# Layer 2's front taken up sequence by sequence behind layer 1, in a four-layer kernel

## The chip, the core and the metric

The kernel runs on one core of a Trainium2 chip. The metric is device time in microseconds (us) of one execution. The engines are PE (TensorE; PEld is its weight load), DVE (VectorE), ACT (ScalarE), POOL (GpSimd) and SP, which here only issues DMAs.

## The reference

The input `x` is 2 sequences of 1024 tokens with 128 features. Four layers run one after the other. Each takes a layer norm of `x`, gives it to two branches, and adds the product of the two to `x`:

```
n = layernorm(x);  x = x + attn(n) * silu(ffn(n))
```

Layer 0 is a Mamba-2 state space branch with dense experts. Layer 1 is a delta-rule recurrence whose output is normalised again (`o`), times a mixture of 8 experts with a shared expert, two experts per token. Layer 2 is a linear attention, times a branch that holds a causal softmax attention over rotated rows with its own RMS norm and a second mixture of 8 experts. Layer 3 is a state space branch in both directions, times experts. The change concerns the end of layer 1 and the front of layer 2:

```
moe, shared = ...                      # layer 1, per token
x  = x + layernorm(o) * silu(moe + shared)
n  = layernorm(x)                      # layer 2
r  = rope(rms_norm(n) * norm1_w)
Q, K, V = r @ Wq, r @ Wk, r @ Wv       # then softmax attention, causal
```

## The kernel before

All of `x` stays on the chip as 16 tiles of 128 tokens by 128 features. Four tiles are a group, so there are groups 0 to 3: groups 0 and 1 are the first sequence, 2 and 3 the second. `LATE` is the order 0, 2, 1, 3, the first halves of both sequences before the second halves.

The kernel is traced through a scheduler that sets each engine's order from dependences and its own estimate of times, except inside `manual_schedule` blocks, where the named engines keep the order in which the code issues. Every engine executes its queue strictly in order. A pool is a region of memory; a pool that is opened where another stood waits for the older one to be released, as a whole, or tile by tile where it has `reuse_waits="tile"`.

**End of layer 1** (`layer1`, from line 924). Expert blocks of 128 rows go through PE; each result is scattered to memory by an indirect DMA on POOL's queue (line 1399). Between blocks PE runs the recurrence: `delta` for the groups in the order of `LATE`, then `scan` tile by tile for both sequences. `close(g)` (1129) normalises the recurrence's output of a group: stats and a Newton root on DVE (`moments`, 354), four scalings on DVE (1133), two POOL operations (1134, 1135). `shared(g)` (990) is the shared expert of a group: four products on PE, Silu on ACT, a product on DVE (1000), two more products, and a copy to `acc` that alternates between ACT and DVE (`copy`, 320). Last, for each group in the order of `LATE`, `fetch` (1404) loads the scattered results back with two DMAs on SP's queue and adds them with eight scaled additions on DVE (`add_scaled`, 484), ACT takes the Silu, and DVE multiplies and adds into `x` (1156, 1157).

**Front of layer 2** (`layer2`, 1160). Its pools are opened after all of layer 1's are released. POOL multiplies the cosine and sine tables with the norm weights (1204). `normalise` (374) does, for each group, stats on DVE, a root as Sqrt on ACT with a reciprocal on DVE (`rsqrt`, 341), four scalings to `xn` (382), four transposes on PE and a copy to `xT`. Then `Attention.prepare` (1535), for each sequence: a second root for the RMS norm, four scalings on ACT to `xw` (1547), six POOL operations for the rotation of each group (1555 to 1560), transposes and a copy to `xrT`; after that five projections of 128x512 and one small one per group on PE. Each projection is cast on ACT to `high` and combined on DVE (`parts`, 1529 to 1533). `softmax_attention` (1705) first makes constants on DVE (1713 to 1719: two 128x128 casts, two 128x512 casts, four memsets). Its loop has PE's order by hand: `maxima` (1592) on banks `pm`, three of them, reduced by DVE (1619), then scores `psc`, exponentials on ACT and products with the values `pat`. A list of other pieces (`routed`, 1223) is threaded into given steps of this loop, for example `hidden_columns` (1187), four transposes and a copy.

**Layer 3** (`Layer3.front`, 1827) already takes each sequence as layer 2 finishes it, with DVE's order by hand. The changed layer 2 has the same shape.

Of the kernel before, what the change touches and what calls it, by code (L numbers as in the profile page):

```python
# [11 lines left out]
F32 = mybir.dt.float32  # L12
# [8 lines left out]
P = 128  # L21
# [4 lines left out]
G = 4  # L26
# [249 lines left out]
class Kern:  # L276
# [77 lines left out]
    def moments(self, pool, src, n, eps, tag, newton=False):  # L354

        nc = self.nc
        mv = pool.tile([P, n, 2], F32, name=tag + "mv", tag=tag + "mv")
        rs = pool.tile([P, n], F32, name=tag + "rs", tag=tag + "rs")
        for j in range(n):
            st = pool.tile([P, 6], F32, name=tag + "st", tag=tag + "st", bufs=4)  # L360
            nc.vector.bn_stats(st, src(j))
            nc.vector.bn_aggr(mv[:, j, :], st)
        if newton:
            self.newton(pool, rs, mv[:, :, 1], 1.0, eps)
        else:
            self.rsqrt(rs, mv[:, :, 1], 1.0, eps)
        return mv, rs
# [556 lines left out]
def layer1(K, x, xn, xT, w, inp):  # L924
    nc, tc, c = K.nc, K.tc, K.c
    four = [P, G, P]
    with ExitStack() as es:
# [4 lines left out]
        sf = es.enter_context(tc.tile_pool(name="sf1", bufs=4, space=PSUM))  # L932
        K.normalise(pf, sf, x, xn, xT, inp["lists"][0])

        with tc.tile_pool(name="r1", bufs=1) as pr:
            m1, m2, hot = K.top2(pr, K.logits(pr, sf, xT, w["wr"], w["br"], 8), 8)
            d = Dispatch(K, pf, pr, sf, hot, 8, P, inp["lists"])
            w12 = K.pair_softmax(pf, K.lead(pf, m1, m2, d.last))
        pe = es.enter_context(tc.tile_pool(name="e1", bufs=1))
# [44 lines left out]
        t13 = pf.tile([P, 2, 256], F32, name="t13")  # L984
        t2 = pf.tile([P, 2, P], F32, name="t2")
# [4 lines left out]
        def shared(g):  # L990
            rhs = xT[:, g * 512 : (g + 1) * 512]
            hT = pe.tile([P, 2, 512], F32, name="hT")
            for k in range(2):
# [4 lines left out]
                sg = pe.tile([P, 512], F32, name="sg")  # L998
                nc.scalar.activation(sg, pgt, AF.Silu)
                nc.vector.tensor_mul(hT[:, k, :], sg, put)  # L1000
# [4 lines left out]
            K.copy(grp(acc, g), po)  # L1005


        big = lambda n: pa.tile([P, NT, P], F32, name=n)
        kn, qT, WT, TV, AT = big("kn"), big("qT"), big("WT"), big("TV"), big("AT")
# [138 lines left out]
        for g in LATE[NB:]:  # L1148
            close(g)
        for g in range(NG):  # L1150
            shared(g)
        K.table, K.users = None, []
        for g in LATE:
            run(d.fetch(pe, acc, g, w12))
            K.act(grp(acc, g), grp(acc, g), AF.Silu)
            nc.vector.tensor_mul(grp(acc, g), grp(acc, g), grp(o, g))
            nc.vector.tensor_add(grp(x, g), grp(x, g), grp(acc, g))


def layer2(K, x, xn, xT, w, inp, last):  # L1160
    nc, tc, c = K.nc, K.tc, K.c
    four = [P, G, P]
    flat = lambda a: a.rearrange("p a b -> p (a b)")
    with ExitStack() as es:
        keep = es.enter_context(tc.tile_pool(name="k2", bufs=1))
        s = keep.tile([P, NT, P], F32, name="s")
        h = keep.tile([P, NT, P], F32, name="h")
        hT = keep.tile([P, T], F32, name="hnT")
        rs = keep.tile([P, NT], F32, name="rs")
        lg = keep.tile([P, NT, 8], F32, name="lg")  # L1170
        r2 = keep.tile([P, NT], F32, name="r2")
        normed = {}

# [19 lines left out]
        with ExitStack() as e1:  # L1193
            pf = e1.enter_context(tc.tile_pool(name="f2", bufs=1))
            K.phase("sqrt_and_others")
            seqs = [Attention(K, pf, xn, w, h, b) for b in range(NB)]
            ms = keep.tile([P, NT], F32, name="ms")
            with tc.tile_pool(name="sn2", bufs=8, space=PSUM) as sn, tc.tile_pool(name="p2", bufs=1) as pp:

                n1 = w["n1"].rearrange("p (f two) -> p f two", two=2)  # L1200
                turn = {}
                for n, a in (("cos", 0), ("sin", 0), ("cos", 1), ("sin", 1)):
                    turn[n, a] = pp.tile([P, TPB, 64], F32, name=f"{n}{a}")
                    nc.gpsimd.tensor_mul(turn[n, a], w[n], n1[:, :, a].unsqueeze(1).to_broadcast([P, TPB, 64]))
                K.normalise(pp, sn, x, xn, xT, None, ms)
                K.rsqrt(r2, ms, 1.0, 1e-5)
                for a in seqs:
                    a.prepare(pp, sn, ms, turn)
            for rate, log in inp["rates"]:
                nc.scalar.activation(rate, log, AF.Exp)  # L1210
# [3 lines left out]
            K.phase("natural_log_exp_and_others")  # L1214
            with tc.manual_schedule(engines={mybir.EngineType.PE}):
                with ExitStack() as e3:
# [10 lines left out]
                    softmax_attention(K, pf, sm, sc, so, seqs, routed)  # L1227
# [290 lines left out]
class Attention:  # L1518
# [6 lines left out]
    def __init__(self, K, pf, xn, w, h, b):  # L1525
        self.K, self.pf, self.xn, self.w, self.h, self.b = K, pf, xn, w, h, b
        self.mT, self.ao = {}, {}

    def parts(self, pp, dst, src, low):

        high = pp.tile([P, 512], F32R, name="high", tag="high", bufs=2)
        self.K.nc.scalar.copy(high, src)
        self.K.nc.vector.scalar_tensor_tensor(dst, high.bitcast(F32), low, src, ALU.mult, ALU.add)

    def prepare(self, pp, sc, ms, turn):
        K, pf, xn, w, b = self.K, self.pf, self.xn, self.w, self.b
        nc, c = K.nc, K.c
        four = [P, G, P]
        xrT = pp.tile([P, SEQ], F32, name="xrT", bufs=2)
        rs = pp.tile([P, TPB], F32, name="ars", bufs=2)  # L1540
        for g in range(TPB // G):
            tiles = range(b * TPB + g * G, b * TPB + g * G + G)
            gr = rs[:, g * G : (g + 1) * G]
            K.rsqrt(gr, ms[:, tiles.start : tiles.stop], 1.0, 1e-6)
            xw = pp.tile(four, F32, name="xw", bufs=2)
            for j, i in enumerate(tiles):
                nc.scalar.activation(xw[:, j, :], xn[:, i, :], AF.Copy, scale=gr[:, j : j + 1])
            pair = xw.rearrange("p t (f two) -> p t f two", two=2)
            xe, xo = pair[:, :, :, 0], pair[:, :, :, 1]
            at = slice(g * G, g * G + G)  # L1550
            cose, sine, coso, sino = (turn[n, a][:, at, :] for a in range(2) for n in ("cos", "sin"))
            xr = pp.tile(four, F32, name="xr", bufs=2)
            t2 = pp.tile([P, G, 64], F32, name="t2", bufs=2)
            t3 = pp.tile([P, G, 64], F32, name="t3", bufs=2)
            nc.gpsimd.tensor_mul(xr[:, :, :64], xe, cose)
            nc.gpsimd.tensor_mul(t2, xo, sino)
            nc.gpsimd.tensor_sub(xr[:, :, :64], xr[:, :, :64], t2)
            nc.gpsimd.tensor_mul(xr[:, :, 64:], xe, sine)
            nc.gpsimd.tensor_mul(t3, xo, coso)
            nc.gpsimd.tensor_add(xr[:, :, 64:], xr[:, :, 64:], t3)  # L1560
            K.to_feature_major(sc, lambda i: xr[:, i % G, :], xrT, g)
        self.qT = qT = pf.tile([P, 4, SEQ], F32R, name="qT", bufs=2)
        self.kT = kT = pf.tile([P, SEQ], F32R, name="kT", bufs=2)
        self.va = va = pf.tile([P, TPB, 4, 32], F32, name="va", bufs=2)
        nc.gpsimd.memset(va, 0.0)
        nc.gpsimd.memset(va[:, :, :, 8], 1.0)
        for g in range(TPB // G):
            cols = slice(g * 512, (g + 1) * 512)
            pk = sc.tile([P, 512], F32, name="pk", tag="ps")
            K.mm(pk, w["wk"], xrT[:, cols])  # L1570
            self.parts(pp, kT[:, cols], pk, w["klow"])
            for j in range(4):
                pq = sc.tile([P, 512], F32, name="pq", tag="ps")
                K.mm(pq, w["wq"][:, j, :], xrT[:, cols])
                self.parts(pp, qT[:, j, cols], pq, w["qlow"])
            pv = sc.tile([P, G, 32], F32, name="pv", tag="ps")
            for j in range(G):
                i = g * G + j
                K.mm(pv[:, j, :], xrT[:, i * P : (i + 1) * P], w["wv"])
            nc.vector.tensor_copy(va[:, g * G : (g + 1) * G, :, :8], pv.rearrange("p t (g d) -> p t g d", d=8))  # L1580
# [124 lines left out]
def softmax_attention(K, pf, sm, sc, so, seqs, fill):  # L1705
# [6 lines left out]
    shared = {n: pf.tile(s, F32R, name=n + "R") for n, s in (("ident", [P, P]), ("ones", [P, P]), ("nge", four), ("nle", four))}  # L1712
    nc.vector.tensor_copy(shared["ident"], c["ident"])
    nc.vector.tensor_copy(shared["ones"], c["ones"])
    for n in ("nge", "nle"):
        nc.vector.tensor_copy(shared[n], seqs[0].w[n].unsqueeze(1).to_broadcast(four))
    shared["mp"] = [pf.tile(four, F32R, name=f"mp{n}") for n in range(4)]
    for t in shared["mp"]:
# [436 lines left out]
```

## Time and profile before

| | us |
|---|---|
| Runs of the kernel | 1321.91, 1326.75, 1313.99; median 1321.91 |
| The profiled execution | 1326.39, of which the traced span is 1324.6 |
| Busy in the span | PE 1139.9, DVE 886.0, ACT 506.4, POOL 386.9 |
| Mean granted clock of PE | 0.913 of full speed |
| Last expert block of layer 1 on PE | ends at 419.7 |
| Last addition into `x` by layer 1 | starts at 453.3 |
| First statistics of layer 2 | 459.1 |
| First projection of layer 2 | 479.8 |
| First product of the softmax attention | 504.9 |

Times in the trace count from the start of the span. A group of rows gives line, engine, operation, tile names, sizes and count; what stands in brackets is idle time before it and what ended it. PE's products of fp32 operands appear as two records each. A busy share is an average over a stretch; the clock column is the share of full speed that PE was granted.

### The profile page before, as it was taken

The numbers are of one execution on the slowest core, as the hardware profiler recorded it, in microseconds if no ns is written. First come the engines' busy times: TensorE is split into PE (matmuls) and PEld (weight loads), VectorE is DVE, ScalarE is ACT, GpSimd is POOL, SyncE is SP. The second block draws the span as 40 slices with busy tenths as digits, with TensorE's granted clock in tenths as the row PEclk, the third lists the DMA queues.
The fourth block names the chain that finished last, engine by engine and source line by source line (L and its number), as shares of the span: only waits on it lengthen the run. The fifth ranks groups of instructions, "written<-read, shape, count | busy, mean of one in ns | idle before, by whom it ended". The sixth has DMA issues, their size and how long they took to land.

```text
span 1324.6 us, 18595 instructions
## 1 busy us (share of the span) xinstructions
PE 1139.9 (86%) x6689; PEld 767.2 (58%) x6689; DVE 886.0 (67%) x2311; ACT 506.4 (38%) x917; POOL 386.9 (29%) x372
## 2 busy tenths in 40 slices
PE   5599986888899468899999998499999849999997
PEld 2257765887898235444444444377778725555554
DVE  7944367954855976576788644869767388653376
ACT  5633334113212251344555676042442236422321
POOL 0073530045643350000000000134656411343433
PEclk9799985899999766797999999699999969999998
DMA  2000003035443100000000000234344430421110
GB/s 92 1 0 1 1 15 127 1 124 158 127 125 107 32 1 1 0 1 0 1 1 17 1 1 17 76 90 129 100 135 132 130 111 1 95 53 48 34 39 24
DMA packets 37804, 71.27 MB, mean 54 GB/s; under 512 B 5275, under 2 KB 22176, under 8 KB 37328
## 3 DMA queue, kind: packets, MB, share of 16 engines
q1 hardware_dynamic: 30880, 54.83, 13.7%
q0 software_dynamic: 5440, 9.79, 2.9%
q10 hardware_dynamic: 1392, 5.47, 1.2%
q8 instruction: 53, 0.87, 0.3%
q14 instruction: 39, 0.32, 0.1%
HBM read 62.58 MB, written 8.85 MB: 54 GB/s over the span
## 4 chain that ended last, share of the span: by engine, by line
PE 66%; DVE 18%; issue 7%; ACT 5%; DMA 2%; POOL 2%; ACTq 0%; SPq 0%; DVEq 0%; POOLq 0%; another core or an unknown queue 0%
PE pm L329 6%; PE psc L329 4%; PE pat L329 4%; PE p L329 4%; DVE mx L1619 4%; PE po L329 3%; PE px L329 3%; PE pgt L329 3%; PE pcum L329 3%; PE psh L329 2%; PE put L329 2%; PE pU L329 2%; PE pd L329 1%; PE pTT L329 1%; PE py L329 1%
## 5 line engine op out<-in xcount | busy, mean ns | idle before, releaser
L1619 DVE TENSOR_REDUCE mx<-pm 128x1 f32<-128x512 f32 (+3 forms) x304 | 185.5, 656 | 76.2 <-PE pm L329 71.7
L1389 POOL DMA_INDIRECT xb<-xs,dfrom x85 | 85.2, 1002 | 503.0 <-PE psum L329 348.3
L292 ACT ACTIVATE pr<-psc 128x1024 f32<-128x1024 f32 x144 | 139.6, 1021 | 101.3 <-PE psc L329 69.1
L329 PE MATMUL pm<-kT,qT 32*128 32x128 f32 (+3 forms) x576 | 110.5, 370 | 7.5 <-DVE mx L1619 6.7
L329 PEld LDWEIGHTS pm<-kT,qT 32*128 32x128 f32 x576 | 68.1, 206 | 78.8 <-DVE mx L1619 51.9
L1399 POOL DMA_INDIRECT ys<-yb,dto x85 | 87.4, 1028 | 81.9 <-DVE yb L1279 50.5
L329 PE MATMUL p<-xbT,tw 128*128 128x256 f32 x368 | 99.7, 387 | 4.5 <-ACT sg L1272 2.6
L329 PE MATMUL pat<-pr,va 128*32 128x512 f32 x576 | 80.9, 634 | 0.9 <-DVE ao L326 0.9
L1272 ACT ACTIVATE sg<-p,tw 128x256 f32<-128x256 f32 x92 | 41.0, 471 | 91.2 <-PE p L329 75.8
L329 PEld LDWEIGHTS p<-xbT,tw 128*128 128x128 f32 x368 | 62.8, 192 | 15.4 <-ACT sg L1272 4.3
L329 PE MATMUL psc<-qT,kT 32*128 32x512 f32 x288 | 64.2, 492 | 3.8 <-ACT pr L292 3.8
L1273 DVE SCALAR_TENSOR_TENSOR hh<-p,tw,sg 128x256 f32<-128x256 f32 x92 | 42.5, 478 | 34.2 <-ACT sg L1272 22.4
L2060 POOL TENSOR_TENSOR hT<-hT,gb 128x512 f32<-128x512 f32 x32 | 41.7, 1303 | 75.9 <-DVE hT L2058 67.1
L329 PEld LDWEIGHTS po<-tw,hh 128*128 128x128 f32 x368 | 54.7, 193 | 9.5 <-issue 4.0
L329 PE MATMUL po<-tw,hh 128*128 128x128 f32 x368 | 56.6, 278 | 0.5 <-DVE hh L1273 0.4
L2058 DVE TENSOR_TENSOR hT<-hT,put 128x512 f32<-128x512 f32 x36 | 24.5, 683 | 47.0 <-PE put L329 46.4
L329 PE MATMUL psc<-mT,onesR 32*128 32x512 f32 x288 | 54.6, 419 | 0.0
L338 PE MATMUL tp<-w_c,xn 128*128 128x128 f32 x48 | 14.5, 412 | 46.7 <-DVE xn L382 46.7
L669 POOL TENSOR_TENSOR uda<-w_c,vdA 128x512 f32<-128x512 f32 x24 | 27.1, 1142 | 88.3 <-PE pd L329 40.8
L292 ACT ACTIVATE hT<-pgt 128x512 f32<-128x512 f32 x36 | 21.3, 596 | 78.5 <-PE pgt L329 70.7
L329 PEld LDWEIGHTS psc<-qT,kT 32*128 32x128 f32 x288 | 31.0, 189 | 16.4 <-ACT pr L292 13.4
L338 PEld LDWEIGHTS tp<-w_c,xn 128*128 128x128 f32 x48 | 8.7, 188 | 53.3 <-DVE xn L382 27.6
(540 smaller groups left out, 2740.5 us busy)
## 6 DMA issues: line engine op xcount, KB each, us to landing
tw<-in_rows SPq DMA_DIRECT2D x23, 836.0 KB
tw<-in_rows SPq DMA_DIRECT2D x39, 384.0 KB
gb<-gt SPq DMA_DIRECT2D x32, 256.0 KB
yt<-ys SPq DMA_DIRECT2D x16, 256.0 KB
w_l<-in_l ACTq DMA_DIRECT2D x1, 1890.0 KB
w_e<-in_e SPq DMA_DIRECT2D x1, 1536.0 KB
xb<-xs,dfrom POOLq DMA_INDIRECT x85
ys<-yb,dto POOLq DMA_INDIRECT x85
```

What stands on the lines that cost most here:

```text
L292: op = self.nc.scalar.activation(out, in_, func, **kw)
L329: op = self.nc.tensor.matmul(out, lhsT=lhsT, rhs=rhs, start=start, stop=stop)
L338: self.nc.tensor.transpose(pt[:, j, :], src(g * G + j), self.c["ident"])
L669: pool.tensor_mul(da, upto.unsqueeze(1).unsqueeze(1).to_broadcast(lay), m["dA"][:, i0 + j : i0 + j + per, :].unsqueeze(3).to_broadcast(lay))
L1272: nc.scalar.activation(sg, p1[:, k - k0, :], AF.Silu, bias=t[:, 1536 + k : 1537 + k])
L1273: nc.vector.scalar_tensor_tensor(hh[:, k, :], p2[:, k - k0, :], t[:, 1540 + k : 1541 + k], sg, ALU.add, ALU.mult)
L1389: self.K.nc.gpsimd.indirect_dma_start(dst, None, self.xs, bass.IndirectOffsetOnAxis(self.of_token[:, n : n + 1], 0))
L1399: d = self.K.nc.gpsimd.indirect_dma_start(self.ys, bass.IndirectOffsetOnAxis(self.to[:, n : n + 1], 0), src, None, bounds_check=2 * T - 1, ...
L1619: nc.vector.tensor_reduce(mx[:, starts.index(a), g, j : j + k], tile[0][:, : k * m].rearrange("p (j m) -> p j m", m=m), AX.X, ALU.max)
L2058: nc.vector.tensor_mul(hT, hT, put)
L2060: nc.gpsimd.tensor_mul(hT, hT, gb[k // 2][:, k % 2, :])
```

## The change

- `layer2` becomes a class `Layer2`. Its `front` is called by `layer1` while layer 1's experts' memory (now on the right side of the memory, with `WT` in it) is still held; the recurrence's pools are released before it (`es.close()`). Four PSUM banks (`sf`) stay layer 1's, the other four become the front's ring `sn`.
- Inside `front`, the order of DVE and POOL is the order of the code. Groups are finished in the order 0, 1, 2, 3 instead of 0, 2, 1, 3, and the statistics, roots, turns and projections of the first sequence are issued between the ends of the second sequence's groups.
- `normed` takes the place of `close(g)` for groups 1 and 3: one Newton root for both, the scaling on ACT with a bias, and the two POOL operations.
- Three roots per token (layer norm, its product with the RMS norm, and one for the linear attention) come from one Newton iteration per sequence over 3x8 values on DVE. The Sqrt table is not loaded. `xw` is made on ACT straight from `x`.
- The rotation of group 3 is on DVE instead of POOL. `xw` and `xr` lie in `h`, the tables in `s`, the turned columns in `hT`.
- The attention's constants move from DVE to ACT (casts) and POOL (memsets) and are issued at the start. Copies of `acc` and of the turned columns are all on ACT. `sg` and `high` get one more buffer.
- The 16 transposes of `xn` and their copies to `xT` move into the attention's loop, at steps 8, 12, 16 and 20.
- `moments` gets two buffers, which also concerns the norms at the start of layers 0 and 1.

```diff
-        mv = pool.tile([P, n, 2], F32, name=tag + "mv", tag=tag + "mv")
-        rs = pool.tile([P, n], F32, name=tag + "rs", tag=tag + "rs")
+        mv = pool.tile([P, n, 2], F32, name=tag + "mv", tag=tag + "mv", bufs=2)
+        rs = pool.tile([P, n], F32, name=tag + "rs", tag=tag + "rs", bufs=2)
...
-        for g in LATE[NB:]:
-            close(g)
-        for g in range(NG):
-            shared(g)
+        es.close()
...
+        def normed():
+            gs = LATE[NB:]
...
+            for k, i in sorted(enumerate(tiles), key=lambda a: a[0] % G):
+                st = pe.tile([P, 6], F32, name="lost", bufs=8)
+                yield lambda st=st, i=i: nc.vector.bn_stats(st, o[:, i, :])
+                yield lambda st=st, k=k: nc.vector.bn_aggr(mv[:, k, :], st)
+            yield from K.newton_steps(pe, r, mv[:, :, 1], 1.0, 1e-5)
...
+                nc.scalar.activation(o[:, i, :], o[:, i, :], AF.Identity, bias=b[:, k : k + 1], scale=r[:, k : k + 1])
...
+            def turned(g, by=nc.gpsimd):
+                a = seqs[g * G // TPB]
...
+                    nc.scalar.activation(xw[:, j, :], x[:, i, :], AF.Identity, bias=shift[:, i : i + 1], scale=factors[:, 1, i : i + 1])
+                a.rotate(pp, xr, xw, g * G % TPB, turn, by)
...
+            with tc.manual_schedule(engines={mybir.EngineType.DVE, mybir.EngineType.Pool}):
+                run(chain(shared(0), shared(1), normed()))
+                run(gather(0))
+                run(gather(1))
+                run(shared(2))
+                run(close(0))
+                run(stats(0))
+                run(close(1))
+                run(stats(1))
+                run(roots(0))
+                turned(0)
+                run(shared(3))
+                turned(1)
+                run(gather(2))
+                run(close(2))
+                run(stats(2))
+                run(gather(3))
+                columns(0, sn)
+                low = projected(0, sn)
+                run(islice(low, 1))
+                run(close(3))
+                run(stats(3))
+                run(roots(1))
+                run(islice(low, 3))
+                columns(1, sn)
+                turned(2)
+                run(scaled(0))
+                turned(3, v)
+                run(low)
+                run(projected(1, sn))
+                columns(2, sf)
+                run(projected(2, sf), scaled(1))
+                columns(3, sf)
+                run(projected(3, sf), scaled(2))
+                run(scaled(3))
+                run(second_root())
+            K.users.append(seqs[-1].cast)
+            K.phase("natural_log_exp_and_others")
...
+                    for g in range(NG):
+                        routed.append((8 + 4 * g, lambda g=g: columns(g)))
...
-    nc.vector.tensor_copy(shared["ident"], c["ident"])
-    nc.vector.tensor_copy(shared["ones"], c["ones"])
+    nc.scalar.copy(shared["ident"], c["ident"])
+    nc.scalar.copy(shared["ones"], c["ones"])
...
-        nc.vector.memset(t.bitcast(F32), 0.0)
+        nc.gpsimd.memset(t.bitcast(F32), 0.0)
```

`run` takes steps of the given lists in turn, one of each. `close(g)` in the list is layer 1's last multiplication and addition of a group, `gather(g)` its eight scaled additions and the Silu. `projected(g)` yields six DVE steps (five results, one copy of the values), each after its product on PE and its cast on ACT; `islice(low, n)` takes the next n of them.

## The prediction

> **What bounds the kernel now.** Three rows of the page's 40 slices (33.1 us each) come first: the share of PE, of VectorE (DVE), and the clock granted to PE.
>
> ```profile
> PE   5599986888899468899999998499999849999997
> DVE  7944367954855976576788644869767388653376
> PEclk9799985899999766797999999699999969999998
> ```
>
> Nearly everywhere PE is at 8 or 9. Slices 13 and 14 (430 to 497 us) read 4 and 6; DVE reads 9 and 7 there and the clock drops. That is where layer 1 hands over to layer 2. The table by 10 us stretches (start:end, length, busy PE, PEld, DVE, ACT, POOL, clock, DMA) shows it closer:
>
> ```profile
> 440.00:450.00 10.00, 4.35 (x22) 2.91 (x20) 9.04 (x22) 1.89 (x4) 3.61 (x2) 0.81 0.09 27
> 450.00:460.00 10.00, 0.00 (x0) 0.00 (x0) 8.98 (x24) 1.91 (x2) 6.65 (x6) 0.50 0.00 0
> 460.00:470.00 10.00, 3.22 (x10) 1.81 (x10) 9.69 (x50) 4.09 (x14) 5.33 (x10) 0.50 0.00 0
> 480.00:490.00 10.00, 10.00 (x25) 4.82 (x26) 5.13 (x8) 5.23 (x12) 4.88 (x7) 0.81 0.00 0
> 490.00:500.00 10.00, 9.76 (x41) 5.68 (x40) 7.37 (x12) 5.28 (x10) 0.00 (x0) 1.00 0.01 2
> ```
>
> DVE is full until 470 while PE stands still; then PE carries the four groups' projections at 480 to 504 (the second after the first, all behind the statistics). The waits from 419 to 505 (who waited for whom, us in total, times, longest) and the time line name the works:
>
> ```profile
> PE tp L338 <- DVE xn L382: 23.0, 7, 14.9
> DVE kT L1533 <- ACT high L1532: 6.2, 4, 3.3
> ```
> ```profile
> 455.54 1.49 DVE L1716 CAST nleR<-w_l 128x512 fp32r<-128x512 f32 x1
> 457.08 2.11 DVE L1719 MEMSET mp<- 128x512 f32 x4
> 468.24 2.20 DVE L382 TENSOR_SCALAR xn<-x,lnmv,lnrs 128x128 f32<-128x128 f32 x3
> 468.25 0.73 POOL L1557 TENSOR_TENSOR xr<-xr,t 128x256 f32<-128x256 f32 x1
> 470.36 0.71 DVE L372 TENSOR_TENSOR ms<-ms,lnrs 128x4 f32<-128x4 f32 x1
> 442.68 2.52 POOL L1134 TENSOR_TENSOR WT<-WT,w_l 128x512 f32<-128x512 f32 x1 [12.04 <-DVE WT L1133]
> 504.92 0.70 PE L329 MATMUL pm<-ngeR,identR 128*128 128x512 f32 x2 [0.94 <-DVE va L1580]
> ```
>
> From 453.9 to 459.1 DVE builds the attention's constants, with layer 2's statistics behind them. Beside a running POOL operation a DVE operation of two SBUF inputs, or a TENSOR_SCALAR from SBUF to SBUF, ends only about when POOL's does: xn at 0.73 each instead of 0.28 (the four at 441.49 took 1.11), a 4-column product at 0.71 instead of 0.15. It goes the other way too: 2.52 instead of 1.08 on POOL. The attention's first product is at 504.92, 0.15 after DVE's last `va`. The forecast is when that product comes.
>
> **The change, step by step.** I walk DVE's hand order with durations from this profile; starts next to each other are counted as pitch (a 128x128 operation 0.28, a 128x512 one 0.65, a small dependent one 0.20, four `bn_stats` and four `bn_aggr` 1.2).
>
> 1. Shared experts of groups 0 and 1, four products. The last `put` ends at 429.2 as before (the bank it needs comes free with a copy at 428.1), so DVE is done at 430.0. In between it idles about 3 us: the norms of layer 1's late groups are behind these products by hand, though their rows are there at 425.7.
> 2. `normed`: eight stats-aggr pairs at about 0.42 and 12 small steps: 3.4 + 2.4, to 435.8. The eight scalings leave DVE (8 x 0.28 = 2.2 saved) for ACT, which has room; then four POOL operations of 1.09.
> 3. `gather` of groups 0 and 1: 16 x 0.28 = 4.5. The results landed at 428.8, no wait. POOL's four operations lie beside it. Each can hold one DVE operation (0 to 4 x 0.8 = 3.2); at 428.8 two cost 1.4, at 442.7 one cost DVE nothing. I take 2.1: 442.4.
> 4. Shared group 2 (1.3), twice close and stats (2 x 2.5), 13 root steps (2.6): 451.3. Layer 3's same list took 13 us from 1064.3 to 1077.3, with 1.2 of other work, which fits.
> 5. Shared group 3, `gather`, close, stats, `gather`: 1.3 + 2.25 + 1.3 + 1.2 + 2.25 = 8.3. POOL turns groups 0 and 1 just then, 12 operations at 0.72. Seven adds at 0.72 instead of 0.28 cost 3.1, the close 1.0, the wait for its Silu 0.9: 464.7. Bounds for the port: 0 and 12 x 0.45 = 5.4.
> 6. One projection result (0.8), close (1.3, 0.5 late behind Silu), stats 1.2, roots 2.7: 471.2. POOL is at rest, so the roots run at 0.20.
> 7. Three results (2.4), four scalings beside POOL's turn of group 2 (4 x 0.72), then group 3's turn on DVE, six operations of 128x256 at 0.42 (between the 128x128 and the 128x512 row): 479.0. Group 0's projection used the four `sn` banks meanwhile; PE waits for these results.
> 8. The rest of group 0 (1.1), group 1 (5 x 0.8 + 0.3), group 2 with four scalings (5.4), group 3 at PE's pace (0.86 each) with scalings (6.0): 495.9. ACT's casts (0.58 each) keep up. The last scalings and the second root (1.5) lie beside PE's first products.
>
> The attention's first product comes at 496.2, 8.7 earlier. Gone besides: constants (5.2 of DVE to ACT and POOL, which are free before 430; without that room they would delay the norms by as much), six of twelve 0.65 us DVE copies. The square root table (1.28) sat in an ACT pause and counts nothing. The exp table now comes after the last cast; the first exponential is 26 us later. POOL's queue has its last store at 420.5, ahead of the constants, so no store is held. On SP's queue the loads of the third group's results go out when the first group's tiles are free (438.6) and are wanted at 452.6; a load issued at 422.8 was used at 428.8, so they are in time.
>
> 9. Moved into the attention: 16 transposes and four copies of xT. The nearest row is the same thing at full clock:
>
> ```profile
> 726.75 0.66 PE L1190 MATMUL tp<-w_c,hn 128*128 128x128 f32 x4
> ```
>
> 0.49 until the next product, 1.0 at half clock, and a bank of three held for a copy of 0.58. Low end 2 us for four, high end 4 x 2.1 if PE waits for the bank each time. Steps 8 to 20 lie at about 560 to 610, partly at half clock: +3.
>
> 10. Two buffers for `moments`. Layer 1's start loads ACT tables six times between 203 and 218 as Sqrt and Silu alternate; the second buffer lets a Sqrt come earlier. Two loads fewer are 2.6 and what waits behind; a poorer order costs about 1. Between -4 and +1: -1.
>
> Sum: -8.7 + 3 - 1 = -6.7. The profiled execution took 1326.4 (span 1324.6 and 1.8 around it), so 1319.7 in its place. The median of the runs shown, 1321.9, is 4.5 lower: 1315.
>
> On step 8, the row for a cold start is the first projection: products start 1.7 apart from 479.8 to about 484, then 0.86, so about 2 us are lost after a pause. The sum has that off its path, since PE starts on group 2 at 477 while DVE turns group 3. The Trainium skill's page "TensorE: Matmul & The Clock Gate" (section "Why this matters for your kernels") speaks against this change: it advises no PE gaps above about 3 us between bursts, as one idle window brings half clock back. By that rule groups 0 and 1, now drawn apart by DVE's results, would run at half clock throughout, and group 2 would start so: an estimate from its window of 3.4 us is 1.7 us lost, and the forecast 1317.
>
> **Rivals.**
>
> *The port is free.* If DVE's runs of adds hold the port and POOL is the one delayed, as at 442.68, the 2.1, 4.1 and 1.8 us of steps 3, 5 and 7 fall away: 8.0 more, 1307. Against it: at 468 POOL ran through at 0.73 and DVE lost each time.
>
> *The attention gives it back.* Its clock stood at 0.50 from 590 to 610; PE did 19.6 us of work there that at full clock is 9.8, with DVE and ACT needing about 12. One such stretch more costs up to 8 us: +1, 1323. For it: the added transposes fall just there. Against it: four at 726 left no trace.
>
> *The tail runs at half clock* (slower than before). PE's products wait for four banks that DVE frees late; if the clock never recovers, from 477 come two turns (1.9 each), three products and a v of group 1 (6.8) and two whole groups (10.2 each): 508.1, a cast and a result more 509.7. That is 4.8 late instead of 8.7 early, with 3 and -1 +6.8: 1329. It decides as soon as the first product comes after 502.9. Against it: 24 us of the same products brought the clock to 1.0 within 5 us.
>
> **How the numbers follow.** Forecast (1309 to 1321) 0.40; port free 0.31; attention gives back 0.13; half clock in the tail 0.16. Port free reaches down to 1303 with step 10 at -4 and step 9 at 2, and to 1300 if DVE's pause of 3 us in step 1 closes as well; half clock reaches up to 1337 with step 9 at 8 and the attention's opening (505 to 510, clock 0.76) at 0.50, 2.5 us. 1300 to 1331 leaves out about 0.1 on each side. A measurement of this kernel can tell about 1% (13 us) from no change. Faster than 1308.7: port free and a little of the forecast, 0.34. Slower than 1335: the upper half of the half clock case, 0.08. Within: 0.58.
>
> **What would show it.** First masked product at 493 to 500 instead of 504.9; no constants on DVE; adds of group 2 at about 0.7 each beside POOL's turns, root steps at 0.2; PE clock low from 445 to about 480, then 1.0; the attention itself 2 to 4 us longer. I would be wrong if ACT's or PE's order, which is not by hand, puts a cast that waits for a bank ahead of a Silu or a turn that DVE waits for, or if other stages are ordered anew.

## The result and the profile after

| | before | after |
|---|---|---|
| Median of 17 runs each, us | 1318.96 | 1328.81 |
| Ratio to before, 95% interval | | 1.0062 (1.0038 to 1.0087) |
| Profiled execution, us (span) | 1326.39 (1324.6) | 1329.81 (1328.0) |
| First statistics of layer 1 | 202.2 | 205.8 |
| First expert block on PE | 279.4 | 271.5 |
| Last expert block on PE begins | 417.8 | 421.2 |
| Last copy of the recurrence's `o` begins | 425.5 | 441.7 |
| Last addition into `x` by layer 1 begins | 453.3 | 479.9 |
| First product of the softmax attention | 504.9 | 511.5 |

The change made the kernel slower, by about 8 us in 1319. The forecast was a gain of 6.7 us. That the median still lies between 1300 and 1331 is luck: that range was stretched upward by a rival whose mechanism is not the one found here.

The three rows of the page, now of the kernel after (PE, VectorE, granted clock, 40 slices of 33.2 us):

```profile
PE   5599996889899577899999998589999939999997
DVE  7944358854864896568888653878777378762466
PEclk9798987689999767589999899699999969999999
```

The hole in PE at the hand-over is still there (slices 13 and 14 read 5 and 7), and the clock still falls. The table by 10 us stretches shows that it has moved (columns as in the prediction):

```profile
430.00:440.00 10.00, 10.00 (x61) 7.37 (x60) 4.58 (x19) 3.39 (x7) 0.00 (x0) 1.00 0.14 39
440.00:450.00 10.00, 1.65 (x10) 1.09 (x8) 8.44 (x23) 2.83 (x9) 6.63 (x9) 0.69 0.00 0
450.00:460.00 10.00, 5.96 (x22) 3.88 (x23) 9.71 (x27) 4.54 (x11) 7.41 (x4) 0.62 0.36 106
480.00:490.00 10.00, 5.69 (x15) 3.18 (x14) 9.55 (x33) 4.83 (x11) 3.61 (x7) 0.74 0.00 0
490.00:500.00 10.00, 8.15 (x23) 3.56 (x21) 7.35 (x13) 4.69 (x8) 1.05 (x2) 0.92 0.00 0
```

From 430 to 440 PE is full and DVE is half idle (4.58; the kernel before had 9.69 in these same 10 us): DVE has nothing it may do. Why, the time line says (start, length, engine, line, operation, tiles; in brackets the idle time before and what ended it):

```profile
441.06 1.64 POOL L1833 MEMSET mp<- 128x512 f32 x3 [13.81 <-PE pO L329]
441.69 0.27 ACT L1120 COPY WT<-pO 128x128 f32<-128x128 f32 x1 [0.16 <-PE pO L329]
442.53 0.20 DVE L308 TENSOR_SCALAR nww<-lomv 128x8 f32<-128x8 f32 x1
442.67 5.00 POOL L1216 TENSOR_TENSOR s<-w_l 128x512 f32<-128x512 f32 x4
442.76 1.22 DVE L314 TENSOR_SCALAR lors<-nww 128x8 int32<-128x8 int32 x1
444.01 1.20 DVE L316 TENSOR_TENSOR nwa<-lors 128x8 f32<-128x8 f32 x1
446.49 1.21 DVE L318 SCALAR_TENSOR_TENSOR lors<-nwa,lors 128x8 f32<-128x8 f32 x1
447.73 0.17 DVE L316 TENSOR_TENSOR nwa<-lors 128x8 f32<-128x8 f32 x1
449.01 1.13 DVE L484 SCALAR_TENSOR_TENSOR acc<-yt,rw,acc 128x128 f32<-128x128 f32 x4
511.53 0.70 PE L329 MATMUL pm<-ngeR,identR 128*128 128x512 f32 x2 [1.16 <-DVE va L1697]
```

The recurrence's last output arrives at 441.7, 20.5 behind the last block (before: 7.7). Only then does POOL get the memory in which `s` and `mp` lie, and its four table products run just beside the Newton steps of the late groups, which take 1.2 each until POOL is done and 0.17 after. The norms end at 449.0 (forecast: 435.8). From there to the first product it takes 62.5; the forecast had 60.4.

So the tail that the prediction walked through was nearly as long as forecast, and it began 13 us too late. What has the recurrence, which the diff does not touch, to do with it? Its place in PE's queue. Here are PE's products behind the last one of the last block, in the order in which PE executes them, up to the last `put` (S: products of the recurrence's scan, H: products of the shared experts):

```
before:  H3 S3 H3 S1 H34
after:   H3 S4 H4 S4 H9 S4 H11 S4 H1 S4 H12
```

Four products of the scan are left behind the last block before, twenty after.

**Theories.** A: the second buffer of `moments` (the forecast's step 10) made the scheduler order PE's work in layer 1 anew; the blocks now come ahead of the recurrence, and its end, with all of DVE's hand order, falls late. B: POOL's tables on the recurrence's memory meet the Newton steps whatever the buffers. C: the front gains what was forecast, and the attention or the clock gives it back.

### The profile page after: what moved, and what is told of

Read it like the earlier page. It is cut to its first block, busy times and chain, and to the rows that moved or that the text cites. A ratio compares the mean times of both kernels' runs of the same rounds, so it can differ in the third digit from the quotient of the medians.

```text
span 1328.0 us, 18567 instructions
## 1 busy us (share of the span) xinstructions
PE 1145.9 (86%) x6689; PEld 772.0 (58%) x6689; DVE 884.0 (67%) x2289; ACT 510.3 (38%) x922; POOL 386.2 (29%) x370
## 4 chain that ended last, share of the span: by engine, by line
PE 67%; DVE 19%; issue 6%; ACT 4%; POOL 2%; DMA 1%; SPq 0%; POOLq 0%; ACTq 0%; DVEq 0%
PE pm L329 6%; PE pat L329 4%; PE psc L329 4%; PE p L329 4%; DVE mx L1736 4%; PE px L329 3%; PE po L329 3%; PE pgt L329 3%; PE pcum L329 3%; PE put L329 2%; PE psh L329 2%; PE pTT L329 2%; PE pU L329 2%; PE pd L329 2%; PE pob L329 1%
## 5 line engine op out<-in xcount | busy, mean ns | idle before, releaser
L1518 POOL DMA_INDIRECT xb<-xs,dfrom x85 | 84.7, 996 | 502.5 <-PE psum L329 370.2
L329 PEld LDWEIGHTS psc<-qT,kT 32*128 32x128 f32 x288 | 30.8, 191 | 15.7 <-ACT pr L292 12.7
L329 PE MATMUL pm<-ngeR,identR 128*128 128x512 f32 x64 | 33.4, 544 | 6.7 <-DVE mx L1736 4.1
L324 ACT COPY xbT<-pxb 128x256 f32<-128x256 f32 (+1 forms) x33 | 12.1, 368 | 68.5 <-PE pxb L963 38.9
```

The costliest lines, as they stand in the source:

```text
L324: self.nc.scalar.copy(out, in_)
L329: op = self.nc.tensor.matmul(out, lhsT=lhsT, rhs=rhs, start=start, stop=stop)
L1518: self.K.nc.gpsimd.indirect_dma_start(dst, None, self.xs, bass.IndirectOffsetOnAxis(self.of_token[:, n : n + 1], 0))
```

## The experiments

All are timed in five rounds against the kernel before. Stages are compared from marks in each profile: the last expert block on PE, the last copy of `o`, the end of the late groups' norms, the last addition into `x`, the attention's first product. Experiments 1 to 4 ran on one chip, 5 to 7 on another, 8 and 9, and 10 and 11, on others again. On the first the blocks were quicker (133 to 143 us instead of 137 to 150), so absolute times are held against each other only within these, and distances from the last block across them. One part of these distances goes with the clock and not with the order: from the last addition into `x` to the first product it took 31.6 us at a clock of 0.89 (the kernel after, experiment 1), 33.3 at 0.85 (experiments 4, 5, 7 and 11), 33.1 at 0.80 (10) and 37.4 at 0.77 (3 and 6).

**1. One buffer in `moments`.** The kernel after, less this:

```diff
-        mv = pool.tile([P, n, 2], F32, name=tag + "mv", tag=tag + "mv", bufs=2)
-        rs = pool.tile([P, n], F32, name=tag + "rs", tag=tag + "rs", bufs=2)
+        mv = pool.tile([P, n, 2], F32, name=tag + "mv", tag=tag + "mv")
+        rs = pool.tile([P, n], F32, name=tag + "rs", tag=tag + "rs")
```

> The kernel after with one buffer instead of two in `moments`; nothing else. PE's issue order up to the recurrence's end is then that of before except for a few pieces. Theory A (the second buffer reorders PE in layer 1, the recurrence ends 16 us late, 441.7 instead of 425.5, and the hand order of DVE stands behind it): the last copy of WT at 425 to 428, the norms of the late groups done at 434 to 438, the attention's first product at 495 to 500, and the kernel 4 to 10 us below before (ratio to before 0.992 to 0.997). Theory B (POOL's table products lie on the recurrence's memory and run beside the Newton steps, whatever the buffers): steps still at 1.2 each, first product at 500 to 503, ratio 0.997 to 1.001. Theory C (the gain is lost in the attention or in a low clock): first product at 495 to 500 but the time still at or above before, ratio 1.003 to 1.008.

Measured: 0.9972 (0.9941 to 1.0003), 0.9% below the kernel after. From its time line:

```profile
412.01 0.26 ACT L1120 COPY WT<-pO 128x128 f32<-128x128 f32 x1
412.73 5.04 POOL L1216 TENSOR_TENSOR s<-w_l 128x512 f32<-128x512 f32 x4
416.56 0.29 DVE L1160 BATCH_NORM_STATS2 lost<-WT 128x6 f32<-128x128 f32 x1
420.05 0.17 DVE L314 TENSOR_SCALAR lors<-nww 128x8 int32<-128x8 int32 x1
422.15 1.13 DVE L484 SCALAR_TENSOR_TENSOR acc<-yt,rw,acc 128x128 f32<-128x128 f32 x4
484.30 0.70 PE L329 MATMUL pm<-ngeR,identR 128*128 128x512 f32 x2 [1.16 <-DVE va L1697]
```

The last block begins at 404.4 here. The last copy is 7.6 behind it, the tables pass beside the statistics, which they do not slow, and are over before the Newton steps. The norms end 17.8 behind the last block (forecast 18.0), the first product comes 79.9 behind it (forecast 78.4; before 87.1; after 90.3). Theory A holds; B is a consequence of the late end; C falls for the larger part.

**2. Two buffers in the kernel before.** The same two lines, the other way round, in the kernel before.

> The kernel before with two buffers in `moments`; nothing else. Theory A: the recurrence ends 10 to 16 us later than 425.5, part of it hidden behind the shared experts and the fetches; the kernel 4 to 12 us slower than before (ratio 1.003 to 1.009). Theories B and C: the buffer does what it was forecast to do, 4 us less to 1 us more (ratio 0.997 to 1.001).

Measured: 1.0076 (1.0043 to 1.0110). With the buffer alone, without any of the rest, the kernel is 10 us longer. Its runs also had a lower clock, 0.905 in the mean against 0.916 before, and by the slope in the last section that much clock goes with the whole 10 us; how much is the order itself, and how much a clock that fell with it, was not separated here. In experiments 3 and 10 the clock was only 0.002 lower, worth 1 to 2 us, and 6.6 and 7.8 us were lost, so the order does cost time by itself. Twenty-eight products of the scan are left behind the last block, the last copy is 31.2 behind it (7.7), the first product 94.8 (87.1).

**3. Two buffers in layer 0's norms only.**

```diff
-        K.normalise(pf, sf, x, xn, xT, None, ms)
+        K.normalise(pf, sf, x, xn, xT, None, ms, bufs=2)   # layer 0; everywhere else 1
```

> The kernel after with two buffers in the norms of layer 0 only, one in layer 1. PE's issue order in layer 1 then differs from before (last product of the recurrence 21 places later, as in after) though layer 1's norms have one buffer. Theory A in the form that only the place of the recurrence on PE counts: ends at 435 to 442, ratio to before 1.000 to 1.008. In the form that layer 1's own two buffers are the cause: ends at 425 to 428, ratio 0.992 to 0.997.

Measured: 1.0050 (1.0017 to 1.0082). Layer 1 has its one buffer, and yet twelve scan products are left behind the last block; the last copy is 17.9 behind it, the first product 93.1. (That is later than the 90.3 of the kernel after, although the last addition is earlier, 55.7 instead of 58.7: the stretch behind it is one of the two at a clock of 0.77.) So it is the place of the recurrence that counts, not layer 1's buffer as such: other times for layer 0 are enough to reorder layer 1.

**4. The additions of groups 0 and 1 ahead of the norms.** Two buffers stay.

```diff
-                run(chain(shared(0), shared(1), normed()))
+                run(chain(shared(0), shared(1)))
                 run(gather(0))
                 run(gather(1))
+                run(normed())
```

> The kernel after with the norms of the late groups (`normed`) behind the additions of groups 0 and 1 in DVE's order instead of ahead of them; two buffers stay. Theory A (DVE's order waits for a recurrence that ends at 441.7): the additions (about 4.5 us) run before 442, the norms end at about 449 as before, and all that follows comes 4 us earlier; first product at 506 to 509 instead of 511.5, 2 to 5 us below the kernel after (ratio to before 1.002 to 1.005). Theory C: first product earlier but the time unchanged, ratio 1.006.

Measured: 1.0045 (1.0011 to 1.0079), first product 89.2 behind the last block. The additions did run while DVE waited, and the last addition into `x` came 55.9 behind the last block instead of 58.7; the first product gained 1.1 on the kernel after, less than the 2.5 to 5.5 expected; the stretch behind the last addition had the lower clock (33.3 us at 0.85 against 31.6 at 0.89). The time lies in theory A's range, but its interval covers theory C's 1.006 too and tells neither from the other.

**5. Two buffers in layer 1's norms only.** As experiment 3, with the call in `layer1`.

> The kernel after with two buffers in the norms of layer 1 only, one in layer 0. PE's issue order in layer 1 is that of after but for a few pieces before the first block. If layer 1's second buffer alone is enough (theory A): the recurrence's last copy 20 us behind the last block, as in after (20.5) and not 7.6 as with one buffer; layer 1's first statistics at 202 to 203 (205.8 in after); ratio to before 1.001 to 1.006. If the loss came from layer 0's end (3.4 us later in three of the four runs with two buffers there): last copy near 8 us behind the last block, ratio 0.994 to 1.000.

Measured: 1.0050 (1.0023 to 1.0076); last copy 20.5, first product 91.0 behind the last block. Each of the two places is enough by itself, and that both together (1.0062) cost more can't be seen within these intervals.

This run and experiment 7 shared a chip, so their stages can be laid side by side. First two buffers in layer 1, then one buffer: from layer 1's first statistics to the first block, to the last block, to the attention's first product.

```profile
202.80:267.60 64.80, 50.94 (x264) 45.31 (x265) 52.21 (x183) 18.32 (x47) 6.64 (x8) 0.68 0.29 95
267.60:414.80 147.20, 137.04 (x1149) 131.69 (x1149) 91.14 (x226) 37.07 (x94) 75.25 (x74) 0.99 0.41 124
414.80:505.80 91.00, 62.22 (x242) 37.33 (x240) 69.77 (x194) 37.33 (x78) 32.89 (x39) 0.83 0.08 24
```
```profile
202.50:278.20 75.70, 60.40 (x360) 53.43 (x361) 60.91 (x197) 21.69 (x51) 8.20 (x10) 0.77 0.25 83
278.20:416.20 138.00, 129.52 (x1085) 124.12 (x1083) 83.63 (x220) 36.61 (x96) 73.75 (x72) 0.99 0.42 131
416.20:497.80 81.60, 58.87 (x209) 33.23 (x207) 63.39 (x186) 36.30 (x74) 32.86 (x39) 0.85 0.09 26
```

The number after PE's busy time counts its records: 264 + 1149 + 242 = 1655 against 360 + 1085 + 209 = 1654. It is the same work. With two buffers the blocks start 10.9 us earlier, 96 records ahead of their old place; 64 of these come back between the blocks, which then take 9.2 longer because PE is full there (137.0 of 147.2), and 33 come back behind the last block. To the last block it is 212.0 against 213.7: of the 10.9, 1.7 are left. The tail is 9.4 longer, since what was put off is a chain at the end of which everything waits.

**6. The blocks held back.** Two buffers stay; on PE the blocks' transposes are placed behind the sixth level of the first recurrence round.

```diff
+                if lv == 5 and side == 1 and "mark" not in loaded:
+                    loaded["mark"] = K.latest
...
-                nc.tensor.transpose(pt[:, r, :], xb[:, r, :], c["ident"])
+                op = nc.tensor.transpose(pt[:, r, :], xb[:, r, :], c["ident"])
+                K.behind(op, loaded["mark"])
```

> The kernel after, two buffers as they are, with one order added on PE: the transposes of the expert blocks come behind the sixth level of the first recurrence round, as they do in the kernel before. On PE three scan pieces, not eighteen, are then left behind the first products of the shared experts. Theory A in the form that the loss is the blocks' start ahead of the recurrence: the last copy 7 to 9 us behind the last block, norms done 17 to 19 behind it, ratio to before 0.996 to 1.003 (PE may lose up to 8 us where it now waits with blocks at hand). In the form that the second buffer costs in another way (layer 0, ACT's tables): last copy early but the time still at 1.004 to 1.009.

Measured: 1.0034 (0.9998 to 1.0069). PE's order at the end is that of before (four products left; the counts of three and eighteen in the expectation were short, it is four and twenty), the last copy 7.7 and the first product 84.7 behind the last block. So the place of the blocks makes the late end. The last addition into `x` came 47.3 behind the last block, a little earlier than with one buffer (48.3, experiment 7). That only some 6 of the 9.4 us of the tail came back lies behind that addition, where the order is as in experiment 7 and the clock was lower: 37.4 us at 0.77 instead of 33.3 at 0.85. The first block came 79.6 behind layer 1's first statistics, 3.9 later than with one buffer. In time the run lies between the two and its interval does not decide; of its 8 us against experiment 7, 3.9 are seen there and 3.1 in the tail, and the rest was not found.

**7. One buffer, and the columns of `xT` late.**

```diff
-                        routed.append((8 + 4 * g, lambda g=g: columns(g)))
+                        routed.append((40 + 4 * g, lambda g=g: columns(g)))
```

> The kernel after with one buffer in `moments` and the sixteen transposes of xn with their copies at the attention's steps 40 to 52 instead of 8 to 20. If they cost about 3 us at steps 8 to 20, where PE was granted half clock (the forecast's step 9): 2 to 4 us less than with one buffer alone (0.9972), so 0.994 to 0.996. If they cost nothing there: 0.997. If they lengthen the stretch at half clock (8 us): 0.990 to 0.992.

Measured: 0.9968 (0.9938 to 0.9999), against 0.9972 with the columns early. What they cost at steps 8 to 20 is not measurable: 3 us (0.0023) are not excluded by these intervals, 8 are hardly likely. This version is below before in its interval, barely, and below the kernel after by 0.9%.

**8. The scalings to `xn` on ACT.** On top of experiment 7, the sixteen scalings leave DVE's order.

```diff
-                    yield lambda i=i: v.tensor_scalar(xn[:, i, :], x[:, i, :], mean[b][:, i - b * TPB, 0:1], factors[:, 0, i : i + 1], ALU.subtract, ALU.mult)
+                    nc.scalar.activation(xn[:, i, :], x[:, i, :], AF.Identity, bias=c0[:, i : i + 1], scale=factors[:, 0, i : i + 1])
```

> One buffer in `moments`, the columns of xT late in the attention, and the sixteen scalings to xn taken from DVE's order and made on ACT behind the last cast, where ACT waits some 26 us for its first exponential. If the front is DVE's own work end to end, as the forecast's steps 3 to 8 have it: the four scalings beside POOL's turn (2.95 in the profile with one buffer) leave the path, and part of the twelve others (0.34 each): the first product 3 to 6 us earlier behind the last block (81.6 with late columns, so 76 to 79), ratio to before 0.992 to 0.995. If the front is bound by something else (PE's pace in groups 2 and 3): 81 behind the last block, ratio 0.997.

Measured: 0.9962 (0.9921 to 1.0002); first product 80.9 behind the last block instead of 81.6. Taking some 7 us of work (2.95 and twelve times 0.34 in experiment 1) from DVE shortened the front by 0.7. The time decides nothing, since its interval covers both expectations, but the stages show that my expectation from steps 7 and 8 failed. The four scalings (2.95) did leave DVE's queue, but its next work, the turn of group 3, then waited 1.40 for POOL and took 4.4 beside it instead of 3.4: 0.6 was left. In the second sequence DVE's scalings lay in the gaps between PE's products.

**9. The late groups' statistics between the shared experts' products.** On top of experiment 8.

```diff
-                run(chain(shared(0), shared(1), normed()))
+                rows = normed()
+                run(chain(shared(0), islice(rows, 16), shared(1), rows))
```

> As the run with xn on ACT, and the sixteen statistics of the late groups' norms stand between the products of the shared experts of groups 0 and 1 in DVE's order instead of behind both. DVE idled 3.0 there in the profile with late columns, and the rows were complete 4.4 us before their statistics began. If that place in DVE's order is what the norms wait for: the norms end 2 to 2.5 us earlier behind the last block (17.8 so far), the two first Newton steps beside POOL's tables at 1.2 instead of 0.2, and the ratio is 0.001 to 0.002 below the run with xn on ACT alone. If PE or POOL holds them: no change.

Measured: the norms end 15.7 behind the last block instead of 17.8, and the first product comes 78.9 behind it instead of 80.9: the 2 us went through to the attention. The time does not show them: 0.9995 (0.9961 to 1.0029) beside 0.9962 (0.9921 to 1.0002). Two us are below what these runs resolve.

**10. POOL's tables behind the norms' scalings.** Two buffers stay; the four table products move behind `normed` in POOL's order.

```diff
                 run(chain(shared(0), shared(1), normed()))
+                tables()
```

> The kernel after, two buffers as they are, with POOL's four table products behind the two scalings of the late groups in POOL's order instead of ahead of them. In the profile of after they ran from 442.7 to 447.7, beside the first Newton steps of the late groups' norms, four of which took 1.2 instead of 0.2. If that meeting costs its 4 us: the norms end 23 to 24 behind the last block (27.5 in after, 17.8 with one buffer), the last addition into x 55 to 56 behind it (58.7 and 48.3), ratio to before 1.002 to 1.004. If the tables only hold other DVE work instead (additions, statistics, roots) or delay the first turn: 1.005 to 1.008.

Measured: 1.0059 (1.0029 to 1.0089), as the kernel after. From its time line:

```profile
440.30 0.17 DVE L314 TENSOR_SCALAR lors<-nww 128x8 int32<-128x8 int32 x1
447.79 1.56 DVE L1178 TENSOR_TENSOR acc<-acc,WT 128x512 f32<-128x512 f32 x1
451.76 5.92 POOL L1217 TENSOR_TENSOR s<-w_l 128x512 f32<-128x512 f32 x4
452.22 1.38 DVE L1178 TENSOR_TENSOR acc<-acc,WT 128x512 f32<-128x512 f32 x1 [0.19 <-issue]
453.63 1.67 DVE L1179 TENSOR_TENSOR x<-x,acc 128x512 f32<-128x512 f32 x1
456.52 1.33 DVE L1236 TENSOR_SCALAR nww<-lnmv 128x8 f32<-128x8 f32 x3
```

The Newton steps are at 0.17 and the norms end 23.7 behind the last block instead of 27.8, as expected; the ratio is that of the second case. But the tables now meet the closing of group 1 (1.38 and 1.67 instead of 0.69 each) and the first root steps (three in 1.33 instead of 0.32). The last addition is 57.3 behind the last block (55 to 56 expected), the first product 90.4: the meeting was moved and not removed.

**11. The recurrence first.** Two buffers stay; every product of the shared experts stands behind the scan's last product on PE, and DVE does the norms ahead of them.

```diff
+        K.ahead = K.latest
         follow(sf, shared, normed, gather, finish)
+        K.ahead = None
...
-                run(chain(shared(0), shared(1), normed()))
+                run(chain(normed(), shared(0), shared(1)))
```

> The kernel after, two buffers as they are, with every product of the shared experts behind the recurrence's last product on PE, and the norms of the late groups ahead of the shared experts' products in DVE's order. PE's order up to the last block is unchanged. If the recurrence ends late because products of the shared experts stand between its last pieces on PE: the last copy 7 to 12 behind the last block instead of 20.5, norms done 17 to 20 behind it (27.5 in after), the last addition into x 50 to 56 behind it (58.7), ratio 0.998 to 1.004; the shared experts end later and may hold the second sequence. If the recurrence's own chain of five steps (two products, a subtraction, two products, an addition) is the length: last copy at 15 or more, ratio 1.004 to 1.010.

Measured: 1.0057 (1.0027 to 1.0086). The last copy is 8.8 behind the last block and the norms end 16.2 behind it, so the shared experts' products did stretch the recurrence. Yet the last addition is 56.2 and the first product 89.5 behind it, and the ratio is above the 0.998 to 1.004 that I expected for this case:

```profile
430.25 1.28 DVE L1001 TENSOR_TENSOR hT<-sg,put 128x512 f32<-128x512 f32 x2
437.68 0.69 DVE L1001 TENSOR_TENSOR hT<-sg,put 128x512 f32<-128x512 f32 x1 [6.15 <-PE po L329]
```

DVE now waits 6.15 for PE's shared experts. With twenty scan products put off, the recurrence or the shared experts come late; none of the three orders behind the last block that were tried (experiments 4, 10 and 11) repaired it.

## Why the prediction was wrong

The steps, against the kernel after and against the kernel with one buffer (experiment 1):

- **Step 10 failed**, in sign and size. It was to give between 4 less and 1 more, taken at -1. It costs 10 us in the kernel before (1.0076) and 0.9%, some 12 us, in the kernel after (1.0062 against 0.9972). Its working was right as far as it went: layer 1's start loads ACT's tables four times instead of six. First before, then after (the last line of each is the last root):

```profile
203.06 1.28 ACT L292 ACT_TABLE_LOAD   x1 [2.39 <-DVE lnst L361]
207.23 1.28 ACT L1023 ACT_TABLE_LOAD   x1
210.23 1.28 ACT L292 ACT_TABLE_LOAD   x1
211.75 1.28 ACT L1023 ACT_TABLE_LOAD   x1
216.20 0.21 ACT L292 ACTIVATE lnrs<-lnrs 128x4 f32<-128x4 f32 x1
```
```profile
206.66 1.28 ACT L292 ACT_TABLE_LOAD   x1 [2.38 <-DVE lnst L361]
209.09 0.20 ACT L292 ACTIVATE lnrs<-lnrs 128x4 f32<-128x4 f32 x1 [0.93 <-DVE lnrs L344]
211.93 0.20 ACT L292 ACTIVATE lnrs<-lnrs 128x4 f32<-128x4 f32 x1 [0.70 <-DVE lnrs L344]
215.32 0.21 ACT L292 ACTIVATE lnrs<-lnrs 128x4 f32<-128x4 f32 x1
```

  The last root comes 9.7 behind the first statistics instead of 14.2. I priced that gain and a "poorer order" of about 1 in layer 1's start, and stopped there. That gain let the blocks go ahead of 96 to 112 of PE's records in front of them, and they started 11.5 us sooner behind layer 1's first statistics (kernel after against before; 10.9 in experiment 5 against 7, 4.3 in experiment 4 against 1). PE has little room from there to the last block (busy 137.0 of 147.2 in experiment 5), and nearly nothing was left at the last block (215.4 against 215.6; 212.0 against 213.7; 202.7 against 201.8): the recurrence was what was put off. The prediction named it in its last sentence ("if other stages are ordered anew") and gave it no price.
- **Step 1** took over the time of the last `put` and of the rows (425.7) "as before". In the kernel after the rows are there 20.5 behind the last block instead of 7.7. With one buffer the step holds.
- **Step 2** had 2.4 for the Newton steps. In the kernel after it was 6.5, since POOL's four table products run beside them. No step has these products; the nearest sentence is the one on the constants, for which it has POOL "free before 430". The late end of the recurrence took that room away, and it cost 4.1. Together with the late rows: norms 27.8 behind the last block, of which 5.9 more than with one buffer come from the rows and 4.1 from the tables.
- **Steps 3 to 8** hold as a sum where the clock behind the last addition was 0.89: 60.4 forecast, 62.5 in the kernel after, 62.1 with one buffer. With the same order in the front it was 63.8 at 0.85 (experiment 7) and 66.8 at 0.77 (experiment 6), which the steps don't have. Inside, errors cancel. The sixteen additions of step 3 took 4.2 (449.0 to 453.2) and POOL waited (3.39 for a 1.09 operation): there DVE was not held and POOL was, as the first rival said. The closing of group 0 took 1.56 and 1.46 instead of 0.65 each. And step 7's scalings did not lie on the path as its sum has them: without all sixteen the front was 0.7 shorter (experiment 8).
- **Step 9** (+3) can't be told from nothing (experiments 1 and 7).
- The front as forecast, without step 10, is 5.7 less than before; measured with one buffer 3.7 and 4.2 (0.9972 and 0.9968, the first interval reaching 1.0003). The front's own part is 7.2 and 5.5 less from the last block to the first product (87.1 to 79.9 and 81.6), where 8.7 was forecast.
- A reading was off by 3: the first exponential starts 29 us behind the last cast in the kernel before (503.8 to 532.9), not 26. Nothing rests on it.

The rivals: *half clock in the tail* named the point from which it decides, a first product after 502.9, and the product came at 511.5, but not through the clock: that was back at 0.92 from 490 to 500 and at 1.0 after. Its price, 6.8 us more, is close to the 8 measured by luck. A weaker form of it is seen in experiments 3 and 6, where the clock of 0.77 made the end of the front 4 to 6 us longer. *The port is free* held for step 3 alone. *The attention gives it back*: from its first product to its last exponential it took 308.0 against 306.1.

On the Trainium skill's page "TensorE: Matmul & The Clock Gate" (section "Why this matters for your kernels"), which the prediction weighed: in the kernel after the clock stood between 0.60 and 0.74 from 440 to 490, while groups 0 and 1 were projected between DVE's results, with pauses of PE of 12.4, 3.8 and 3.6 us, and was back for groups 2 and 3 (no pause over 1.7 from 490 to 510). That agrees with its rule on gaps between bursts, though the clock was not at half throughout, as the prediction had worked out. In the attention the rule does not hold the clock: in the kernel before it fell from 1.00 to 0.50 between 588 and 590 with no pause over 0.44 in the ten us before, and the last section has a longer case.

## What to carry to other kernels

An edit in a helper is an edit in every stage that calls it, and where a scheduler sets the order, in every stage behind. Before pricing the hand-written part, lay the instruction order of the untouched stages beside the old one: here twenty scan products instead of four behind the last block would have pointed at the loss before any run. And an earlier start is a gain only if the engine that does the work has room; on an engine that is nearly full it chooses what will be late, and here the late piece was the one that the whole next stage waits for.

## What was not expected of the hardware

**The opening of the attention stays at half clock with PE almost full.** From the kernel of experiment 8 (10 us stretches; the clock is third from the end):

```profile
520.00:530.00 10.00, 9.40 (x35) 6.23 (x35) 5.75 (x14) 2.50 (x3) 0.00 (x0) 0.50 0.01 2
530.00:540.00 10.00, 9.36 (x48) 5.38 (x49) 3.78 (x9) 3.14 (x5) 0.00 (x0) 0.50 0.00 0
540.00:550.00 10.00, 9.36 (x57) 4.52 (x54) 6.08 (x14) 3.19 (x4) 0.00 (x0) 0.50 0.00 0
550.00:560.00 10.00, 9.04 (x41) 3.81 (x34) 5.76 (x10) 2.89 (x4) 0.00 (x0) 0.50 0.01 2
```

PE is busy over 90% there and the clock does not rise. It had fallen from 1.00 (498 to 500) to 0.50 (502 to 504), and from 500 to 560 no pause of PE is longer than 0.78 us. In the kernel of experiment 9, which differs by 2 us in when it gets there and has pauses up to 0.78 from 500 to 520 too, it is at 0.67 and more from 520 on. Over the thirteen profiles the length of the attention goes with the clock that it lost: with (1 - clock) x length between 17.9 and 40.9 us, it is 298.7 to 314.7 us long, 0.63 us for each us lost, with 1.1 us of scatter, whichever variant it is. This is most of why 2 us can't be resolved in a kernel of 1310: over 32 runs of the kernel before on one chip, 0.01 of mean clock goes with 9 us of time, and what is left scatters by 1.9. What sets how soon the clock comes back was not tried.

**A small dependent DVE step beside POOL costs the whole POOL operation.** The prediction had this for a 4-column product (0.71 beside a POOL operation of 0.73); beside longer POOL operations it costs more. A 128x8 step took 1.20 to 1.23 beside a 128x512 product of POOL and 0.17 without, while statistics beside the same product stayed at 0.26 to 0.29. The Trainium skill's page "GPSIMD Engine Reference" (section "1. Specifications") says that POOL's SBUF interfaces are shared with VectorE, with contention for instructions in a 2-port mode or with two SBUF inputs; the Newton steps with two inputs agree with that, and the TENSOR_SCALAR of one input (1.22) was held just as long; whether it ran in a 2-port mode no run here shows. Here it is a factor of seven, and four such steps cost 4.1 us.
